# Another order for the hand-written statements of a fused cross-attention kernel: start, steady loop and end

## The chip, the core and the metric

The kernel runs on one core of a Trainium2 chip. The metric is the device time of one execution in microseconds (us); the median of three runs of the kernel before is 1369.0 us (1368.85 to 1369.27). Four compute engines matter: TensorE (PE: matrix products, with its weight loads shown apart as PEld), VectorE (DVE), ScalarE (ACT) and GpSimd (POOL). SyncE (SP) issues all the DMA transfers that are spoken of here. Each engine works through its own list of instructions in order and waits on semaphores for the others.

## What is computed

There are 64 independent batches, all in float32. In each, 256 rows of text `x` (512 wide) attend to 256 rows of context `c` (384 wide):

```python
text_p  = x @ W_text  + b_text              # 256 x 512
audio_p = c @ W_audio + b_audio             # 256 x 512
Q = layer_norm(text_p, g1, beta1)
K = layer_norm(audio_p, g2, beta2)
V = audio_p
alpha = softmax(Q @ K.T / sqrt(512))
h = (alpha @ V) @ W_out + b_out
out = layer_norm(h + x, g_out, beta_out)
```

## The kernel before, in words

**Work per batch.** The kernel saves products of matrices with Strassen-like schemes: blocks of the operands are added and subtracted ahead of the products, and the products are combined in PSUM. The sums that feed products are made on POOL, the combinations in PSUM on DVE and ACT. The weight W_out is folded into W_audio at the start (`fold_multiply`, `fold_evict`), so that `alpha @ c` is multiplied by one folded weight (`wao`).

Four kinds of work make up a batch:

- Keys: class `Thirds`, lines 559 to 731. The product of the context block and W_audio is cut into thirds and done as 15 products in five groups, `one()` to `five()`. Between them lie small steps in PSUM: after `one()`, ACT copies one result (`copy_n1`, line 608), DVE subtracts it from the other and leaves that in the bank of `T` (`start_t`, line 612), and only then can PE accumulate there (`three()`, line 595). Likewise `copy_t`, `start_l0` and `start_l1` stand between `three()` and `four()`, and `take_m` and `start_u` between `four()` and `five()`. `five()` accumulates in its third group of products on the `M0` that `start_u` has to have read.
- Queries: class `Pair`, lines 840 to 944, two batches at a time, with seven outer and seven inner products each. POOL makes the sums: `sum(1)` to `sum(4)` (line 857, 128x512 each), `side(m, 0)` (128x256), `side(m, 1)` and `side(m, 2)` (128x128; line 866).
- Scores and softmax: class `Attention`. `key_sums` and `query_sums` list the sums of the transposed keys and queries, `key_step(n)` and `query_step(n)` (lines 1016 and 1019) do them on POOL; `key_step(0)` is one 128x512 operation of POOL. Then `score_part`, `maxima`, `exponentials`, `reciprocals`, `divide_e`.
- Context and output: `context_part` and `context_two` (`alpha @ c`), then a second `Thirds` object, called `y` or `y1` in the loop, with the folded weight. It ends in `plus_ends`, `plus_middle`, `plus_n0` and the four sums `last_11`, `last_10`, `last_01`, `last_00` (lines 686 to 731) on DVE, which add `x` and leave totals for the layer norm of the output. That layer norm is `totals` (POOL), `deviation` (ACT), `shift` (DVE, line 1428), and `settle` (DVE, line 1439) for one half of the rows; the other half goes through `scale_row` (ACT) and `lift_rows` (POOL).

**Way through DRAM.** Normalised keys and queries and the exponentials are stored to DRAM (`store`, `store_e`), fetched back in squares of 32 (`fetch`, `fetch_e`) and transposed block by block on DVE (`turn`, `turn_e`). The inputs come in squares too (`load_c`, `load_x`) and are turned by `turn_c` and `turn_x`. The DMAs all stand in SP's list.

**Order.** Nothing schedules this kernel: it runs under a manual schedule, and the order of the Python statements is the order of the instructions on every engine. Lines 1482 to 2207 are the start (batches 0 to 3, with other forms of the same steps, among them class `Fork` for the queries), lines 2209 to 2569 the steady loop, and lines 2571 to 3050 the end (batches from 60 on). The loop `for b in range(4, B - 4, 2)` runs 28 times, and each round treats two batches at each stage of the pipeline; its first half is written with `k2`, `y`, `f`, `at`, `settled`, its second with `k21`, `y1`, `s`, `at1`, `settled1`. In the middle of a round, from line 2344 (`y.five()`) to line 2398 (`k21.three()`), the following stand among each other:

- on PE: `y.five()`, four `last.context_part`, `k21.one()`, two `s.multiply`, `k21.two()`, `old1.context_two(0)`, `s.multiply(1, 6)`, `k21.three()`;
- on DVE: `y.plus_ends`, `plus_middle`, `last_11`, `plus_n0`, `last_10`, `plus_middle`, `last_01`, `settled.settle(0)`, `y.last_00`, `k21.start_t()`;
- on POOL: `s.sum(1)`, `s.side(1, 0)`, `s.sum(2)`, `s.sum(3)`, `s.side(1, 1)`, `s.side(1, 2)`, `at1.query_step(0)`, `s.sum(4)`, and, after `k21.three()`, `att[b + 1].key_step(0)`.

The step that is spoken of most:

```python
def settle(self, t):
    nc.vector.scalar_tensor_tensor(
        self.y[:, t, :], self.y[:, t, :], self.r[t], beo_sb, ALU.mult, ALU.add
    )
```

Its two tensor inputs, the row `y` and `beo_sb`, lie in SBUF, as do those of `shift`. The small DVE steps of `Thirds` named above read at least one operand from PSUM.

Of the kernel before, what the change touches and what calls it, by code (L numbers as in the profile page):

```python
# [22 lines left out]
def kernel(  # L23
# [1525 lines left out]
    wa_blocks = third_weights(wa_sb, wa_t, [3])  # L1549
    xs_1 = SumX(xT.pop(1), nc.vector)  # L1550
    fold_multiply(0, 0, 1)
    centre(wt_sb, mean_wt, DC)
    xs[1] = xs_1
    wt_pairs = wt_blocks = weight_sums(wt_sb, DC // 2, 'wtsum')
    q[0].evict(1)
    g1_sb, be1_sb, g2_sb, be2_sb, bac_sb = take_columns()
# [3 lines left out]
    load_c(2)  # L1560
    q[1] = Fork(1, xs.pop(1).of, wt_blocks)
    k[1].evict(0)
    load_x(2)
    fold_multiply(0, 1, 2)
    load_c(3)
    fold_multiply(1, 1, 2)
    k[1].evict(1)
    third_weights(wa_sb, wa_t, [1], nc.vector)
    q[0].scales()
    Fork.seed()  # L1570
    k[1].square()
    cT[2] = turn_c(2)
    q[0].normalise([1])
    xs_1.add(1)
    q[0].normalise([0])
    fold_multiply(0, 2, 3)
    q[1].one()
    cs[2] = Sides(cT.pop(2), 'csum')
    xs_1.add(1)
    fold_multiply(0, 3, 4)  # L1580
    xT[2] = turn_x(2)
    k[1].scales()
    fold_evict(0)
    cs[2].add(1)
    third_weights(wa_sb, wa_t, [4], nc.vector)
    cs[2].add(1)
    q[1].seven()
    cs[2].add(1)
    load_x(3)
    q[1].after_one()  # L1590
    nc.vector.tensor_scalar(be2_sb, be2_sb, scale, None, ALU.mult)
    cT[3] = turn_c(3)
    cs[2].add(1)
    fold_multiply(1, 2, 3)
    q[0].store()
    q[1].two()
    cs[3] = Sides(cT.pop(3), 'csum')
    fold_multiply(2, 0, 1)
    cs[2].add(1)
    k[0].fetch()  # L1600
    ba_delta = third_bias(ba_sb, 'ba_delta')
    load_c(4)
    part = bias_parts()
    cs[2].add(1)
    cs[2].add(1)
    q[1].after_seven()
    cs[3].add(1)
    xs[2] = SumX(xT.pop(2))
    k[1].normalise([1])
    q[0].fetch()  # L1610
    q[1].six()
    k2_0 = k[2] = Thirds('k', 2, cs.pop(2), wa_blocks, ba_sb, ba_delta)
    q[1].after_six()
    inner_step(7, 0)
    fold_multiply(1, 3, 4)
    xs[2].add(1)
    fold_evict(1)
    k2_0.one()
    xs_1.add(1)
    k2_0.copy_n1()  # L1620
    Thirds.seed_with(ba_sb)
    q[1].five()
    bias_rest(part, 1, 2)
    nc.vector.tensor_scalar(g2_sb, g2_sb, scale, None, ALU.mult)
    k2_0.start_t()
    k[1].normalise([0])
    q[1].four()
    load_c(5)
    cs[3].add(1)
    q[1].after_five()  # L1630
    xs[2].add(1)
    k2_0.three()
    xs[2].add(1)
    at_0 = att[0] = Attention(0)
    cs[3].add(1)
# [48 lines left out]
    at_0.affine_keys(0)
    k[1].fetch()
    k2_0.copy_u()
    q[1].fetch()
    k2_0.leave_middle()
    at_0.affine_queries(2)
    nc.vector.tensor_tensor(both[:, 0], g1_sb, g2_sb, ALU.mult)  # L1690
    at_0.affine_queries(0)
    k2_0.middle_d()
    fold_bias(part)
    at_0.affine_queries(3)
    k2_0.leave_ends()
    q2_0.five()
    load_x(4)
    xs[3].add(1)
    k2_0.seed()
    k2_0.leave()  # L1700
    q2_0.after_five()
    k[1].turn([0])
    third_weights(wao_sb, wao_t, [1])
    at_0.affine_keys(2)
    k2_0.square(var_0[:, 2:], [0])
    cs[4] = Sides(cT.pop(4), 'csum')
    load_x(5)
    k2_1 = k[3] = Thirds('k', 3, cs.pop(3), wa_blocks, ba_sb, ba_delta)
    k2_0.middle_sum()
    at_0.score(0, 1)  # L1710
    k[1].turn([1])
    xs[3].add(1)
    q2_0.four()
    xs[3].add(1)
    q[3] = Fork(3, xs.pop(3).of, wt_blocks)
    k2_0.square(var_0[:, 2:], [1])
    k2_1.one()
    q2_0.two()
    cs[4].add(1)
    q2_1 = q[3]  # L1720
    k2_1.copy_n1()
    k2_1.start_t()
    q2_0.three()
    q[1].turn()
    xT[4] = turn_x(4)
    at_0.score(1, 2)
    cs[4].add(1)
    q2_0.square(var_0[:, :2], [0])
    at_0.score(2, 3)
    cs[4].add(1)  # L1730
    k2_1.three()
    at_0.score(3, 4)
    at_0.score(4, 5)
    q2_0.square(var_0[:, :2], [1])
    at_0.score(5, 6)
    at_0.score(6, 7)
    scales_of(q2_0, k2_0, var_0)
    q2_0.normalise([1])
    q2_0.normalise([0])
    load_c(6)  # L1740
    k2_1.two()
    cs[4].add(1)
    at_0.score(7, 8)
    last_1.maxima()
    q2_0.store()
    Fork.seed()
    cs[4].add(1)
    cs[4].add(1)
    at_1 = att[1] = Attention(1)
    k2_0.normalise([0])  # L1750
    k2_1.copy_t()
    k2_1.start_l0()
    k2_0.normalise([1])
    q2_1.seven()
    k2_1.start_l1()
    last_1.exponentials([0])
    q2_1.one()
    var = small.tile([P, 4], F32, tag="var4", name="var")
    at_1.affine_keys(3)
    inner_step(6, 0)  # L1760
    q2_1.after_one()
    inner_step(5, 0)
    k2_1.four()
    xs[4] = SumX(xT.pop(4))
    cs[4].add(1)
    k2_1.take_m()
    k2_0.store()
    last_1.exponentials([1])
    at_1.affine_keys(1)
    q2_0.fetch()  # L1770
    at_1.affine_queries(2)
    last_1.reciprocals()
    k2_2 = k[4] = Thirds('k', 4, cs.pop(4), wa_blocks, ba_sb, ba_delta)
    q2_1.six()
    at_1.affine_queries(0)
    q2_1.after_seven()
    xs[4].add(1)
    k2_1.start_u()
    k2_1.five()
    at_1.affine_keys(0)  # L1780
# [72 lines left out]
    at_1.reciprocals()
    at_2.affine_keys(1)
    at_2.affine_queries(2)
    k2_2.four()
    wao_blocks = third_weights(wao_sb, wao_t, [[0, 3], [4, 2]][1])
    xs[5] = SumX(xT.pop(5))
    k2_2.take_m()
    beo_sb = row(beta_out, 'beo')  # L1860
    old_2.context_two(0)
    load_x(6)
    old_2.context_two(1)
    inner_step(7, 2)
    old_2.copy_two()
    at_2.affine_queries(1)
    q2_2 = q[4]
    old_2.zsides.add(1)
    q2_2.one()
    q2_2.after_one()  # L1870
    at_2.affine_queries(0)
    settled, old, last = att.pop(0), att[1], att[2]
    k2_1.store()
    at_2.affine_keys(0)
    k2_2.start_u()
    q2_1.store()
    load_c_rows(1)
    k2_2.five()
    old_2.zsides.add(1)
    old_2.zsides.add(1)  # L1880
    q2_1.fetch()
    q2_2.seven()
    k2_2.copy_n()
    cT[6] = turn_c(6)
    at_2.affine_keys(2)
    q2_2.two()
# [1198 lines left out]
```

## Time and profile before

| | |
|---|---|
| median of 3 runs | 1369.0 us |
| the profiled execution | 1369.55 us |
| its span, first to last instruction | 1367.8 us |
| PE busy | 1341.2 us, 8839 products |
| DVE busy | 1236.8 us, 3191 instructions |
| ACT busy | 1209.4 us, 3391 instructions |
| POOL busy | 1192.1 us, 1745 instructions |
| granted TensorE clock | 0.999 |
| moved by DMA | 322.25 MB, mean 236 GB/s |

"Busy" is the union of an engine's instructions; matrix products overlap in a pipeline, so a product of float32 with 128 columns shows 275 ns although the next one starts after some 112 ns. Every float32 product shows as two records. A timeline row gives the start in us from the beginning of the span, the length, the engine, the line of the kernel, the operation, the operands (output<-inputs), the shapes and the count of merged instructions; in brackets stands the idle time of the engine before it and what ended it. The line is often that of a helper: L557 is every small DVE step in PSUM, L573 every product of a `Thirds`, so the operands tell them apart.

### The profile page before, as it was taken

To read this page: it belongs to the slowest core of one execution; us is meant where nothing else is said; L and a number is where in the kernel's file an instruction comes from. 1 tells how busy PE (TensorE), PEld (TensorE's weight loads), DVE (VectorE), ACT (ScalarE), POOL (GpSimd) and SP (SyncE) were. 2 spreads that over 40 slices of the span, in tenths; PEclk is the share of its full clock that TensorE was granted. 3 is DMA by queue.
4 is the path that set the end of the run, shared out by engine and by line. 5 is a ranking of instruction groups with operands and counts; after the bars stand their busy time and mean duration, and the time that the engine had idled before them with its cause. 6 is when DMAs were issued, how large, how long until landed. Compare 5 with 4: busy or idle time off the path is not lost.

```text
span 1367.8 us, 30175 instructions
## 1 busy us (share of the span) xinstructions
PE 1341.2 (98%) x8839; PEld 1249.3 (91%) x8839; DVE 1236.8 (90%) x3191; ACT 1209.4 (88%) x3391; POOL 1192.1 (87%) x1745
## 2 busy tenths in 40 slices
PE   9999999999999999999999999999999999999998
PEld 5798999999999999999999999999999999999986
DVE  6668999999999999999999999999999999999977
ACT  4888989999899989899989999989999898999895
POOL 5798988988998988988989889889889889889865
PEclk9999999999999999999999999999999999999999
DMA  9988788998888988889888889988889888889863
GB/s 217 232 235 229 211 226 241 250 248 233 225 254 245 253 244 238 225 251 233 247 257 233 233 239 250 244 239 238 235 239 252 243 241 228 247 238 242 244 214 130
DMA packets 448970, 322.25 MB, mean 236 GB/s; under 512 B 153765, under 2 KB 381349, under 8 KB 448806
## 3 DMA queue, kind: packets, MB, share of 16 engines
q1 hardware_dynamic: 448710, 320.20, 84.7%
q8 instruction: 71, 1.16, 0.4%
q14 instruction: 93, 0.76, 0.2%
q10 hardware_dynamic: 96, 0.13, 0.0%
HBM read 203.57 MB, written 116.65 MB: 234 GB/s over the span
## 4 chain that ended last, share of the span: by engine, by line
PE 73%; ACT 19%; issue 2%; DVE 2%; DMA 2%; POOL 1%; SPq 0%; DVEq 0%; ACTq 0%; POOLq 0%
PE ps_f L889 12%; PE ps_m L573 11%; PE ps_f L906 11%; PE ps_sc L1035 9%; PE ps_z L1175 8%; PE ps_n L573 7%; PE ps_u L573 7%; PE ps_l L573 4%; ACT junk L938 4%; ACT kr L504 3%; ACT qr L944 2%; ACT junk L476 2%; PE ps_f L749 2%; ACT e L1097 2%; PE ps_sc L974 1%
## 5 line engine op out<-in xcount | busy, mean ns | idle before, releaser
L368 POOL TENSOR_TENSOR csum<-csum,cT 128x256 f32<-128x256 f32 (+1 forms) x310 | 213.2, 696 | 7.4
L1175 PE MATMUL ps_z<-eT,c 128*128 128x256 f32 x768 | 196.8, 379 | 0.0
L873 POOL TENSOR_TENSOR xsums<-xsums 128x128 f32<-128x128 f32 (+1 forms) x261 | 143.6, 550 | 51.1 <-PE ps_f L889 48.5
L1175 PEld LDWEIGHTS ps_z<-eT,c 128*128 128x128 f32 x768 | 135.6, 190 | 10.3
L889 PE MATMUL ps_f<-wt_inner,xsums 128*128 128x128 f32 x696 | 137.2, 279 | 0.9 <-DVE ps_f L557 0.5
L543 ACT ACTIVATE qT<-qT,both 128x256 f32<-128x256 f32 x236 | 134.3, 593 | 0.0
L1035 PE MATMUL ps_sc<-kT,qT 128*128 128x128 f32 x928 | 131.9, 275 | 0.0
L1035 PEld LDWEIGHTS ps_sc<-kT,qT 128*128 128x128 f32 x928 | 121.4, 192 | 0.1
L889 PE MATMUL ps_f<-wtsum,xsums 128*128 128x128 f32 x696 | 120.3, 275 | 0.0
L889 PEld LDWEIGHTS ps_f<-wt_inner,xsums 128*128 128x128 f32 x696 | 111.9, 190 | 8.6 <-DVE ps_f L557 1.1
L906 PE MATMUL ps_f<-wt,X 128*128 128x256 f32 x464 | 114.6, 380 | 0.0
L889 PEld LDWEIGHTS ps_f<-wtsum,xsums 128*128 128x128 f32 x696 | 106.3, 191 | 6.0 <-DVE ps_f L557 0.7
L1431 DVE SCALAR_TENSOR_TENSOR yr<-yr,nm,go 128x512 f32<-128x512 f32 x124 | 109.6, 884 | 0.0
L1035 PE MATMUL ps_sc<-ksum,qsum 128*128 128x128 f32 x696 | 105.9, 275 | 0.0
L1035 PEld LDWEIGHTS ps_sc<-ksum,qsum 128*128 128x128 f32 x696 | 95.6, 192 | 1.4
L557 DVE TENSOR_TENSOR ps_l<-ps_m,t 128x171 f32<-128x171 f32 x248 | 84.0, 339 | 10.8 <-ACT t L621 3.0
L1241 ACT ACTIVATE junk<-yr,nm 128x512 f32<-128x512 f32 x124 | 89.8, 724 | 2.8 <-POOL nm L1223 1.8
L1020 POOL TENSOR_TENSOR qsum<-qT 128x256 f32<-128x256 f32 x118 | 86.6, 734 | 4.4 <-ACT qT L543 4.4
L504 ACT ACTIVATE kr<-kr,rstd 128x512 f32<-128x512 f32 x126 | 87.3, 717 | 1.9
L906 PEld LDWEIGHTS ps_f<-wt,X 128*128 128x128 f32 x464 | 81.5, 191 | 7.5
L1017 POOL TENSOR_TENSOR ksum<-kT 128x512 f32<-128x512 f32 x59 | 87.2, 1478 | 0.0
L368 POOL TENSOR_TENSOR csum<-cT 128x256 f32<-128x256 f32 (+1 forms) x124 | 86.0, 694 | 0.0
(322 smaller groups left out, 4666.0 us busy)
## 6 DMA issues: line engine op xcount, KB each, us to landing
kd<-kr SPq DMA_DIRECT2D x64, 512.0 KB, 3.8
qd<-qr SPq DMA_DIRECT2D x64, 512.0 KB, 2.8
kq<-kd SPq DMA_DIRECT2D x256, 128.0 KB, 3.4
qq<-qd SPq DMA_DIRECT2D x256, 128.0 KB, 3.3
xq<-in_x_dram SPq DMA_DIRECT2D x252, 128.0 KB, 3.7
x<-in_x_dram SPq DMA_DIRECT2D x63, 512.0 KB, 5.4
out_dram<-yr SPq DMA_DIRECT2D x62, 512.0 KB, 6.4
cq<-in_ctx_dram SPq DMA_DIRECT2D x252, 96.0 KB, 2.6
```

Of the source, the lines that this page charges most:

```text
L368: nc.gpsimd.tensor_tensor(*step)
L504: nc.scalar.mul(row, row, self.r[t])
L543: nc.scalar.activation(self.T[:, k, :], self.T[:, k, :], AF.Identity, bias=bet[:, k : k + 1], scale=gam[:, k : k + 1],)
L573: nc.tensor.matmul(place, lhsT=self.sides.of[n], rhs=self.weights[n], start=(n == 14), stop=True, skip_group_check=True,)
L873: nc.gpsimd.tensor_tensor(o, i0, i1, ALU.subtract)
L889: nc.tensor.matmul(self.place(m, i, j), lhsT=side, rhs=wt_parts[m][n], start=False, stop=True, skip_group_check=True)
L906: nc.tensor.matmul(bank[:, i], lhsT=self.sides[m][:, i, c], rhs=wt_pairs[m][c], start=False, stop=True, skip_group_check=True,)
L1017: nc.gpsimd.tensor_tensor(*self.ksteps[n])
L1035: nc.tensor.matmul(self.place(t, m), lhsT=self.qsides[n][:, c], rhs=self.ksides[n][:, c], start=False, stop=True, skip_group_check=True,)
L1175: nc.tensor.matmul(ps, lhsT=c_rows[self.b][:, s, bass.ts(j, P)], rhs=self.eT[:, s, :], start=start, stop=(s == ST - 1), skip_group_check=True,
L1241: nc.scalar.activation(junk, self.y[:, t, :], AF.Square, bias=self.nm[:, t : t + 1], accum_out=self.ssq[:, t : t + 1],)
L1431: nc.vector.scalar_tensor_tensor(row, row, self.nm[:, t : t + 1], go_sb, ALU.add, ALU.mult)
```

## The change

The statements of the start from line 1550 on, of the loop and of the end stand in another order. No statement is added, dropped or altered: the 360 statements of the loop are the same ones, 337 of them at another place, and buffers, transfers and shapes stay. The core of the diff, for what the prediction names (the middle of a round, the place before `k2.five()`, and the start):

```diff
@@ the loop, first half: between k2.four() and k2.five() @@
-        old.z_step(7)
+        cs[b + 3].add(1)
+        settled.shift(1)
+        at.open_scores()
+        at1.affine_both(0)
+        f.plus(5, 1)
+        f.multiply(5, 4)
+        settled.last_deviation()
+        k2.take_m()
+        settled.shift(0)
+        f.multiply(5, 3)
+        k2.start_u()
+        k2.five()
...
@@ the loop, the middle of a round, as it stands after @@
+        y.five()
+        last.context_part(0, 0)
+        at.maxima()
+        y.plus_ends(x_old)
+        s.side(1, 0)
+        last.context_part(1, 0)
+        y.plus_middle(x_old, 1)
+        y.last_11()
+        y.plus_n0()
+        s.sum(3)
+        s.side(1, 1)
+        s.sum(1)
+        s.sum(2)
+        y.last_10()
+        last.context_part(0, 1)
+        last.context_part(1, 1)
+        settled.settle(0)
+        y.plus_middle(x_old, 0)
+        k21.one()
+        y.last_01(x_old)
+        k21.copy_n1()
+        s.multiply(1, 1)
+        s.multiply(1, 7)
+        s.side(1, 2)
+        att[b + 1].key_step(0)
+        y.last_00()
+        s.sum(4)
+        k21.two()
+        old1.context_two(0)
+        at.reciprocals()
+        s.multiply(1, 6)
+        k21.start_t()
+        k21.three()
...
@@ the start, as it stands after @@
+    q[0].evict(1)
+    wt_pairs = wt_blocks = weight_sums(wt_sb, DC // 2, 'wtsum')
+    xs_1.add(1)
+    q[0].evict(0)
...
+    k[1].evict(1)
+    cT[2] = turn_c(2)
+    Fork.seed()
...
+    fold_multiply(0, 1, 2)
...
+    fold_multiply(1, 1, 2)
...
+    q[1].seven()
```

Among the DMAs of the loop, `load_x_rows(b - 1)` goes from the head of a round to its first half, `load_x(b + 6)` from the second half to the first, `k2.fetch` from before `k21.copy_n1` to after `k21.five`, and `at.store_e` to behind `q[b + 2].fetch`; `last.turn_e` (DVE) goes from behind `y.five` to before `y.four`.

More of the change, by code (lines that the diff above doesn't have):

```diff
@@ L1566 @@
+    cs[2].add(1)
     fold_multiply(1, 1, 2)
-    k[1].evict(1)
+    k[1].square()
     third_weights(wa_sb, wa_t, [1], nc.vector)
[L1569 to L1573, printed above, removed]
-    xs_1.add(1)
[L1575 to L1583, printed above, removed]
+    ba_delta = third_bias(ba_sb, 'ba_delta')
@@ L1584 @@
+    xs_1.add(1)
     cs[2].add(1)
     third_weights(wa_sb, wa_t, [4], nc.vector)
[L1586 to L1599, printed above, removed]
+    q[0].normalise([1])
     k[0].fetch()
-    ba_delta = third_bias(ba_sb, 'ba_delta')
@@ L1702 @@
-    k[1].turn([0])
-    third_weights(wao_sb, wao_t, [1])
+    cs[3].add(1)
     at_0.affine_keys(2)
[L1705 to L1708, printed above, removed]
     k2_0.middle_sum()
     at_0.score(0, 1)
-    k[1].turn([1])
[L1712 to L1718, printed above, removed]
-    cs[4].add(1)
@@ L1720 @@
[L1720 to L1732, printed above, removed]
+    q2_0.after_six()
+    k2_0.seed()
+    q2_0.five()
+    last_1 = att[0]
+    q2_0.four()
+    k[1].fetch()
+    cs[4] = Sides(cT.pop(4), 'csum')
+    q2_0.two()
+    var_1 = small.tile([P, 4], F32, tag='var4', name='var')
+    q2_0.after_five()
@@ L1861 @@
[L1861 to L1878, printed above, removed]
+    q2_2.after_one()
+    cs[5].add(1)
+    k2_2.five()
+    q2_2.seven()
+    q2_2.six()
@@ L1956 @@
-    old_2.o.start_u()
+    cs[5].add(1)
+    at_2.score(7, 8)
+    old_2.o.start_l0()
+    q2_2.square(var_2[:, :2], [1])
+    old_2.o.four()
+    scales_of(q2_2, k2_2, var_2)
+    att[3] = Attention(3)
+    at = att[3]
+    old_2.o.take_m()
+    var = small.tile([P, 4], F32, tag="var4", name="var")
+    q2_2.normalise([1])
+    k2_2.normalise([1])
+    xs[5].add(1)
+    old_2.o.start_u()
+    Fork.seed()
+    go_sb = row(g_out, 'go')
+    load_x(7)
+    old_2.o.five()
+    cs[5].add(1)
+    at_2.maxima()
@@ L2022 @@
-    k2.two()
-    q2.five()
-    k2.copy_t()
-    k2.start_l0()
-    k2.start_l1()
-    att[3].key_step(0)
-    at.query_sums()
+    k2.two()
+    old.copy_one()
+    k2.copy_t()
+    q2.after_six()
+    settled.totals()
+    k2.start_l1()
+    k2.start_l0()
+    q2_2.store()
+    old.copy_two()
+    settled.deviation(1)
+    q2.five()
+    settled.deviation(0)
+    old.z_step(0)
+    k2_2.fetch()
+    at.query_step(1)
+    k2.four()
+    at_2.divide_e([1])
+    at_2.store_e()
+    at.query_step(0)
@@ new lines @@
+        k2.copy_n1()
+        at.affine_both(1)
+        k2.start_t()
+        old.copy_two()
+        settled.totals()
+        f.multiply(5, 7)
+        f.spread(5)
+        f.keep(5)
+        if b + 4 < B: load_c(b + 4)
+        f.whole(4, 0)
+        k2.three()
+        old.copy_one()
+        q[b + 1].turn()
+        k2.copy_t()
+        f.multiply(5, 6)
+        at.affine_both(3)
+        f.plus(5, 0)
+        settled.deviation(1)
+        k2.two()
+        f.whole(4, 1)
+        att[b + 1] = Attention(b + 1)
@@ L2387 @@
-        s.side(1, 2)
-        k21.start_t()
+        s.sum(3)
+        k2.seed()
+        s.side(1, 1)
+        s.sum(1)
+        s.sum(2)
+        att[b + 1].key_sums()
+        y.last_10()
+        last.context_part(0, 1)
+        last.context_part(1, 1)
+        s.seed(1)
+        settled.settle(0)
+        at.exponentials([0])
+        y.plus_middle(x_old, 0)
+        k21.one()
+        y.last_01(x_old)
+        at.exponentials([1])
+        q[b + 2].store()
+        k21.copy_n1()
+        s.multiply(1, 1)
@@ L2454 @@
-        s.keep(6)
-        old1.z_step(4)
+        k2.fetch()
+        s.multiply(6, 7)
+        q[b + 3].store()
+        k21.copy_n()
+        s.keep(6)
+        cT[b + 4] = turn_c(b + 4)
+        at1.score_part(1, 7)
+        at1.query_step(1)
+        old1.z_step(4)
+        s.spread(6)
+        settled1.shift(1)
+        s.whole(2, 1)
+        k21.copy_u()
+        k21.leave_ends()
+        k21.leave_middle()
+        cs[b + 4] = Sides(cT.pop(b + 4), "csum").add(0)
+        k21.middle_v()
@@ new lines @@
+    k2.two()
+    var = small.tile([P, 6], F32, tag="var6", name="var")
+    old.product_sums()
+    f.multiply(5, 7)
+    at.query_sums()
+    at.affine_both(2)
+    k2.three()
+    f.side(5, 1)
+    at.affine_both(1)
+    k2.copy_t()
+    cT[B - 1] = turn_c(B - 1)
+    f.spread(5)
+    f.whole(4, 0)
+    f.keep(5)
+    q[B - 3].turn()
+    old.context_two(1)
+    settled.deviation(1)
+    cs[B - 1] = Sides(cT.pop(B - 1), "csum").add(0)
+    att[B - 3] = Attention(B - 3)
+    f.multiply(5, 6)
@@ L2914 @@
+    old.o.four()
+    settled_m3.store()
+    settled.shift(1)
+    last.start_products('csum', work, n=0)
+    at.reciprocals()
     old.o.take_m()
-    last.zsides.add(1)
-    settled_m3.store()
     old.o.start_u()
@@ L2919 @@
     at.context_two(0)
[L2920 to L2927 removed]
+    last.copy_two()
+    settled.shift(0)
+    q[B - 1].affine(g1_sb, be1_sb, [2])
+    at.context_one()
+    end = Attention(B - 1)
+    last.zsides.add(1)
+    old.o.plus_ends(x_rows[B - 4])
+    last.o.seed()
+    old.o.last_01(x_rows[B - 4])
+    old.o.plus_middle(x_rows[B - 4], 1)
@@ L2928 @@
+    last.zsides.add(1)
+    at.copy_one()
+    old.o.plus_n0()
+    k2_m3.fetch()
+    old.o.last_10()
+    settled.last_deviation()
+    last.zsides.add(1)
+    last.zsides.add(1)
+    last.o.two()
+    old.o.last_11()
+    at.context_two(1)
+    end.k.turn()
+    old.o.plus_middle(x_rows[B - 4], 0)
+    last_rows(B - 1)
+    old.o.last_00()
+    last.zsides.add(1)
+    last.o.one()
     at.copy_two()
+    end.affine_keys(0)
     last.zsides.add(1)
-    settled.last_deviation()
-    end = Attention(B - 1)
@@ L2932 @@
-    last.o.seed()
-    at.start_output()
-    old.o.last_10()
-    at.reciprocals()
-    at.copy_one()
-    last.zsides.add(1)
-    old.o.plus_middle(x_rows[B - 4], 0)
-    old.o.last_11()
-    settled.shift(0)
-    last.o.two()
-    last.zsides.add(1)
-    end.k.turn()
-    last.o.one()
-    old.o.last_01(x_rows[B - 4])
-    last.o.copy_n1()
-    at.multiply(0, bank[5])
-    end.affine_keys(0)
-    old.o.last_00()
-    end.score(0, 1)
-    end.start_output('kq')
-    end.affine_keys(3)
-    settled.settle(1)
@@ new lines @@
+    add_bias(B - 1, [1])
+    settled.settle(0)
+    last.o.copy_n1()
+    last.o.start_t()
+    settled.settle(1)
+    end.affine_keys(2)
+    old.deviation(0)
+    end.affine_keys(1)
+    last.o.three()
+    end.score(0, 1)
+    last.o.copy_t()
+    old.shift(0)
+    last.o.start_l1()
+    end.score(1, 2)
+    end.score(2, 3)
+    end.affine_keys(3)
+    last.o.start_l0()
+    old.deviation(1)
+    old.last_deviation()
+    old.shift(1)
+    last.zsides.add(1)
+    settled.store()
+    end.start_output('kq')
```

1906 lines of the change are left out of this document (896 added, 1010 removed).

## Prediction

> **What bounds the kernel now.** I read the page first, then the waits of PE, then the timeline of one round on each engine.
>
> ```profile
> span 1367.8 us, 30175 instructions
> PE 1341.2 (98%) x8839; PEld 1249.3 (91%) x8839; DVE 1236.8 (90%) x3191; ACT 1209.4 (88%) x3391; POOL 1192.1 (87%) x1745
> ```
>
> PE is busy for 98% of the span, so an order can gain only what PE loses between its products. The other three have about a tenth of idle time each, so none covers a delay of the others for long. How much PE loses is not seen in "busy", since overlapping products hide short gaps. I take the spacing of products that follow each other without a wait:
>
> ```profile
> 622.26 1.89 PE L1175 MATMUL ps_z<-eT,c 128*128 128x256 f32 x8
> 623.99 0.81 PE L573 MATMUL ps_n<-wa,csum 128*128 128x171 f32 x4
> ...
> 629.07 0.74 PE L573 MATMUL ps_m<-wa_thirds,csum 128*128 128x171 f32 x4
> 629.65 0.74 PE L573 MATMUL ps_l<-wa_thirds,cT 128*128 128x171 f32 x4
> ...
> 610.39 0.61 PE L1035 MATMUL ps_sc<-ksum,qsum 128*128 128x128 f32 x4
> 610.84 0.39 PE L889 MATMUL ps_f<-wtsum,xsums 128*128 128x128 f32 x2
> ```
>
> From start to start, 256 columns take 1.73/8 = 0.216 us, 171 columns 0.58/4 = 0.145, 128 columns 0.45/4 = 0.112. A round has 120 records of the thirds (4 objects with 15 products, two records each), 48 of 256 columns (12 for `whole`, 12 for the context, two each) and 112 of 128 columns (28 inner products of the queries, 28 of the scores, two each): 17.4 + 10.4 + 12.5 = 40.3 us. What a round takes, and where the rest goes:
>
> ```profile
> 599.75 0.51 DVE L557 TENSOR_TENSOR n<-ps_m,x 128x342 f32<-128x342 f32 x1 [0.29 <-PE ps_m L573]
> 601.48 0.33 DVE L557 TENSOR_TENSOR u<-ps_u,x 128x171 f32<-128x171 f32 x1
> 601.73 0.50 DVE L723 SCALAR_TENSOR_TENSOR yr<-ps_l,x 128x342 f32<-128x342 f32 x1
> 602.15 1.85 DVE L1440 SCALAR_TENSOR_TENSOR yr<-yr,rstd,beo 128x512 f32<-128x512 f32 x1
> 603.93 0.32 DVE L723 SCALAR_TENSOR_TENSOR yr<-ps_u,u 128x170 f32<-128x170 f32 x1
> 604.36 0.34 DVE L557 TENSOR_TENSOR ps_u<-ps_n,n 128x171 f32<-128x171 f32 x1
> ...
> 641.29 0.51 DVE L557 TENSOR_TENSOR n<-ps_m,x 128x342 f32<-128x342 f32 x1 [0.29 <-PE ps_m L573]
> ```
>
> The first and the last row are `y.plus_ends` of two rounds running: 641.29 - 599.75 = 41.54 us. A round loses 41.54 - 40.3 = 1.24 us, and 28 rounds lose 35 us. Nearly all of it is one wait:
>
> ```profile
> PE ps_u L573 <- DVE ps_u L557: 17.2, 28, 0.6
> ...
> 603.76 0.39 PE L889 MATMUL ps_f<-wt_inner,xsums 128*128 128x128 f32 x2
> 604.76 0.56 PE L573 MATMUL ps_u<-wa_thirds,csum 128*128 128x171 f32 x2 [0.61 <-DVE ps_u L557]
> 605.16 0.59 PE L1175 MATMUL ps_z<-eT,c 128*128 128x256 f32 x2
> ```
>
> It comes 28 times, once a round: `k21.three()` waits for `k21.start_t()`. The last product before it starts at 603.76 and takes 2 x 0.112, so `three()` could start at 603.98; it starts at 604.76, 0.78 late, and its two records take 0.40 instead of 0.29, 0.11 more. That is 0.89 of the 1.24 us, or 24.9 us in all rounds. The rest, 0.35 us a round, is spread over short gaps.
>
> The DVE rows say why `start_t` (604.36) is late. DVE starts `plus_ends` when PE releases it (599.75) and works without a break up to `start_t`; the one long row is `settled.settle(0)`, 1.85 us. Other rows of the same operation are far shorter, and POOL shows what the long one meets:
>
> ```profile
> L1440 DVE SCALAR_TENSOR_TENSOR yr<-yr,rstd,beo x62: 720/968/1879, 125.0 to 1344.9; 128x512 f32<-128x512 f32 x62
> ...
> 601.50 0.73 POOL L1020 TENSOR_TENSOR qsum<-qT 128x256 f32<-128x256 f32 x1
> 602.19 1.27 POOL L864 TENSOR_TENSOR X<-X,xsums 128x512 f32<-128x512 f32 x1
> 603.42 1.72 POOL L1017 TENSOR_TENSOR ksum<-kT 128x512 f32<-128x512 f32 x1
> ```
>
> The shortest, median and longest `settle` are 0.72, 0.97 and 1.88 us. The long one lies over POOL's `s.sum(4)` (602.19, next operation at 603.42), and DVE goes on at 603.93, 0.51 after POOL's next start, and the POOL operation that starts at 603.42 takes 1.72 us instead of about 1.28. So the two take turns: `settle` waits for the POOL operation in flight, then POOL's next one waits for `settle`. Which POOL operation is in flight when `settle` comes decides whether PE waits.
>
> **The change part by part.**
>
> *The middle of a round, 28 times.* PE's work from `y.five()` to `k21.three()` is the same list in nearly the same order, and so is DVE's between `plus_ends` and `start_t`: `settle` stands two steps earlier, behind `last_10`, and `reciprocals` is added. The order of POOL is new, and these are the rows to place it:
>
> ```profile
> 636.32 1.24 DVE L77 STREAM_TRANSPOSE X<-xq 128x1024 f32<-128x1024 f32 x1
> ...
> 637.70 1.28 POOL L864 TENSOR_TENSOR xsums<-X 128x512 f32<-128x512 f32 x1 [0.20 <-DVE X L77]
> 638.93 0.73 POOL L873 TENSOR_TENSOR xsums<-X 128x256 f32<-128x256 f32 x1
> 639.62 1.28 POOL L864 TENSOR_TENSOR xsums<-X,xsums 128x512 f32<-128x512 f32 x1
> 640.85 1.29 POOL L864 TENSOR_TENSOR xsums<-X 128x512 f32<-128x512 f32 x1
> ...
> 622.93 0.46 POOL L368 TENSOR_TENSOR csum<-csum,cT 128x128 f32<-128x128 f32 x1
> 623.35 0.46 POOL L368 TENSOR_TENSOR csum<-cT 128x128 f32<-128x128 f32 x1
> ```
>
> POOL starts its sums when `turn_x(b + 5)` ends, at 637.70, which is 641.29 - 637.70 = 3.59 before `plus_ends`; `turn_x` hangs on `y.one()`, and PE's list from there to `y.five()` is unchanged, so I keep that distance. Start to start, a 128x512 sum takes 1.23, a 128x256 one 0.69, a 128x128 one 0.42. In the new order `side(1, 0)`, `sum(3)`, `side(1, 1)`, `sum(1)`, `sum(2)`, `side(1, 2)` come first: 0.69 + 3 x 1.23 + 2 x 0.42 = 5.22, so `key_step(0)` starts 5.22 - 3.59 = 1.63 after `plus_ends`, in the frame of the rows above at 601.38; as `sum(2)` reads what `sum(1)` has just written, up to 0.1 later. `settle` takes the place behind `last_10`, 601.48. So `key_step(0)` is in flight first, by 0 to 0.1 us. It is of the size of the sums, so POOL's next start is at 601.43 + 1.23 = 602.66, and DVE goes on 0.51 later, at 603.17. Then come `plus_middle` (601.73 - 601.48 = 0.25), `last_01` (602.15 - 601.73 = 0.42), `last_00` to `start_t` (604.36 - 603.93 = 0.43, into whose gap `reciprocals` goes, with 0.03 over) and `start_t` to `three()` (604.76 - 604.36 = 0.40): 604.70. That is 0.06 earlier than 604.76, and 28 x 0.06 = 1.7 us gained.
>
> The Trainium skill, in SBUF — State Buffer, section "Who interferes with whom", says that a DVE operation with two SBUF inputs and a POOL operation that reads SBUF exclude each other, and that the one which starts first holds the ports for the whole instruction. The turns above agree with the first half. On the second, the rows have `settle` at 602.15 ahead of the sum at 602.19, and yet the sum went first; by the rule on these starts, the same 0 to 0.1 us would decide here.
>
> *Ahead of `k2.five()`.* `start_u` has to have read `M0` before the third product of `five()`:
>
> ```profile
> 630.11 0.74 DVE L1431 SCALAR_TENSOR_TENSOR yr<-yr,nm,go 128x512 f32<-128x512 f32 x1
> 630.76 0.34 DVE L557 TENSOR_TENSOR ps_u<-ps_m,m 128x171 f32<-128x171 f32 x1
> ...
> 630.68 0.75 PE L573 MATMUL ps_n<-wa_thirds,csum 128*128 128x171 f32 x4
> 631.26 0.74 PE L573 MATMUL ps_m<-wa_thirds,cT 128*128 128x171 f32 x4
> ```
>
> `start_u` ends at 631.10 and the third product starts at 631.26: a cover of 0.16 us today. The new order puts `z_step(3)` ahead of the two `shift`, and the sums of POOL against which the `shift` take turns are others. The `shift` at 630.11 frees DVE after 0.65, so it met nothing; against a POOL operation of 0.73 it may take up to 0.7 more, or nothing. Less the cover, the cost is 0 to 0.55 us a round; I take 0 for the likeliest case, the nearest row being this one, and keep the other end as a rival.
>
> *The rest of the loop.* `k21.one()` still follows `last_10` over the same products and keeps its short gap. The new neighbour of the round's end, `k2.one()` behind `last_10` of `y1`, has 7 groups of PE work (4 x 0.432 + 3 x 0.224 = 2.4 us) for a DVE chain that took 601.48 - 599.75 = 1.73 and has `plus_middle` (0.25) and two small steps more: about 2.2, hidden by 0.2. If a stretched `settle` ahead of it eats that, it costs a few tenths; this belongs to the rival with `shift`. `turn_e` before `y.four()` instead of after `y.five()` frees DVE time that ends in its wait for PE (0.29 at 599.75), so it brings nothing.
>
> *SP's list.* Transfers move past each other: `k2.fetch` goes behind `q[b + 2].store`, `at.store_e` behind a fetch of four issues, and `load_x(b + 6)` waits in front of `load_c(b + 5)` until `turn_x(b + 4)` has freed its buffer. The tightest way, store, fetch and turn of the exponentials, has this room today:
>
> ```profile
> 612.21 2.50 SPq L74 DMA_DIRECT2D eq<-ed x4
> ...
> 620.16 0.70 DVE L77 STREAM_TRANSPOSE eT<-eq 128x512 f32<-128x512 f32 x1
> ```
>
> The fetch is issued by 614.71 and turned at 620.16, 5.4 us later. I cost the moves at nothing under this cover; if it goes, DVE waits in front of the turn, and everything queued behind that on DVE with it, from `maxima` to the sums that PE waits for.
>
> *The start and the end.* The start loses two longer waits:
>
> ```profile
> 30.18 0.59 ACT L745 COPY ps_f<-bt 128x512 f32<-128x512 f32 x1 [1.35 <-DVE kr L465]
> ...
> 35.16 1.13 PE L749 MATMUL ps_f<-wt,X 128*128 128x256 f32 x4 [0.52 <-ACT ps_f L765]
> 41.63 0.53 PE L573 MATMUL ps_u<-wa_thirds,csum 128*128 128x171 f32 x2 [0.45 <-DVE ps_u L557]
> ```
>
> Both, 0.52 and 0.45 us and their slow first products, may go, since other work stands around them. But `q[1].seven()` now comes after only two `fold_multiply`, and it needs `Fork.seed`, which needs `k[1].evict(1)`; DVE has `xs_1.add(1)` in front of that in place of one eviction. So PE may wait there for up to about the 1.35 us that ACT waited for the same release, or for nothing. Bounds for the start: 1.5 gained to 1.5 lost, taken at 0. The end has the same products and the same last chain of layer norm; I take it at 0 with 1 us to each side.
>
> **The sum.** From the profiled execution's 1369.55 us (1.75 outside the span of 1367.8): 1369.55 - 1.7 = 1367.85. The median of the runs stands 0.55 lower, so the forecast is 1367.3, rounded 1367.0. Its own range is 1362 to 1373: 0.06 +- 0.1 us a round is 3 us to either side, and the start and the end add 2.5.
>
> **The rivals.** *Settle goes first (0.32).* If `settle` comes a tenth earlier against POOL, or POOL a tenth later, `key_step(0)` waits and `settle` takes its 0.72. Then `three()` could start at 601.48 + 0.72 + 0.25 + 0.42 + 0.43 + 0.40 = 603.70, before 603.98: the wait vanishes, and 28 x 0.89 = 24.9 us go. Some of it returns, since DVE then has less room elsewhere; I take 1.0 of it back: 1345, range 1341 to 1352. For it speaks that the margin is of the size of my rounding; against it, that in the old order the sum won although its row starts 0.04 after `settle`'s.
>
> *DVE is late at `start_u` (0.27).* The price is the stretch of a `shift` above the cover of 0.16 us, in front of `k2.five()` and, in the same way, of `y1.five()`; it decides from the point at which a `shift` or `settle` ahead of them meets a POOL operation with more than 0.16 us to run. At 0.35 us a round for both places together, a third of their 2 x 0.55, it is 28 x 0.35 = 9.8 us: 1367 + 10 = 1377, slower; range 1372 to 1384. For it: DVE is busy 90% and its stretches alone set the old wait. Against it: today's `shift` at that place met nothing.
>
> *The order changes nothing that PE sees.* Then 1369.0; this lies in the likeliest case's range, as the gain of 1.7 us is within what can be told.
>
> **How the numbers follow.** A measurement of this kernel can tell about 0.2%, 2.7 us, from no change. The likeliest case has 0.38: 0.12 faster, 0.21 within, 0.05 slower. The first rival's 0.32 is all faster; the second's 0.27 is 0.25 slower, 0.02 within; 0.03 is left for a wait that I do not see, slower. So faster 0.44, same 0.23, slower 0.33. The range leaves out about a tenth at the low end of the first rival and a tenth at the high end of the second: 1343 to 1379.
>
> **What would show it.** In the profile after, the row of PE waits for `ps_u` from DVE stays at 28 times and near 0.6 us each, and a long `settle` (about 1.7 us) lies over POOL's `ksum<-kT` of 128x512. If that row of waits is gone and the `settle` takes 0.7 to 1.0, the first rival holds. If new PE waits for `ps_m` behind DVE `ps_u` stand in `five()`, the second does. The forecast is wrong in its base if the rounds are equally long and the time differs: then the start or the end did it.

## The result, and the profile after

The new order takes 1390.7 us (median of 4 runs, 1390.2 to 1392.9), the old one 1368.9 (1368.8 to 1369.3): 1.62% slower, ratio 1.0162 with a 95% interval of 1.0144 to 1.0179. Nothing was added, and the granted clock is the same (0.999 and 1.000); the 21.8 us come from the order alone.

First the page after:

```profile
span 1388.4 us, 30050 instructions
...
PE 1356.2 (98%) x8839; PEld 1252.0 (90%) x8839; DVE 1257.2 (91%) x3191; ACT 1216.8 (88%) x3391; POOL 1185.4 (85%) x1745
```

PE and DVE are each "busy" longer, by 15.0 and 20.4 us, over the same instructions. An instruction that stands waiting inside its own record counts as busy. The share of PE, 98% before and after, tells nothing.

The waits of PE (us in total, times, longest):

```profile
PE ps_u L573 <- DVE ps_u L557: 20.9, 29, 1.1
```

This is the old wait, `k21.three()` behind `k21.start_t()`, 17.2 us before. It grew by 3.7 us, and no other row stands above 1.0 us. 28 of its 29 times are the rounds (0.74 us in the one shown below, 0.61 in the one of before); the 29th, 0.33 us, lies in the end. So this view misses most of the loss: it counts only time in which no product's record is open. The `settle` rows show more (shortest, median and longest in ns):

```profile
L1440 DVE SCALAR_TENSOR_TENSOR yr<-yr,rstd,beo x62: 741/1853/1877, 122.4 to 1361.4; 128x512 f32<-128x512 f32 x62
```

The median was 968 ns and is 1853: now both settles of a round are long. The timeline of DVE over one round (start, length):

```profile
691.45 0.51 DVE L557 TENSOR_TENSOR n<-ps_m,x 128x342 f32<-128x342 f32 x1 [0.47 <-PE ps_m L573]
...
693.17 1.85 DVE L1440 SCALAR_TENSOR_TENSOR yr<-yr,rstd,beo 128x512 f32<-128x512 f32 x1
694.95 0.32 DVE L557 TENSOR_TENSOR u<-ps_u,x 128x171 f32<-128x171 f32 x1
695.19 0.50 DVE L723 SCALAR_TENSOR_TENSOR yr<-ps_l,x 128x342 f32<-128x342 f32 x1
...
695.74 0.34 DVE L723 SCALAR_TENSOR_TENSOR yr<-ps_u,u 128x170 f32<-128x170 f32 x1
...
695.99 0.16 DVE L1107 RECIPROCAL rden<-den 128x2 f32<-128x2 f32 x1
696.18 0.34 DVE L557 TENSOR_TENSOR ps_u<-ps_n,n 128x171 f32<-128x171 f32 x1
...
709.38 1.87 DVE L1440 SCALAR_TENSOR_TENSOR yr<-yr,rstd,beo 128x512 f32<-128x512 f32 x1
711.17 0.29 DVE L557 TENSOR_TENSOR ps_f<-ps_f,i 128x128 f32<-128x128 f32 x1
711.37 0.32 DVE L557 TENSOR_TENSOR m<-ps_m,bao_delta 128x171 f32<-128x171 f32 x1
711.62 0.67 DVE L557 TENSOR_TENSOR v<-ps_f,v 128x512 f32<-128x512 f32 x1
712.21 0.33 DVE L557 TENSOR_TENSOR ps_u<-ps_m,m 128x171 f32<-128x171 f32 x1
...
733.79 0.51 DVE L557 TENSOR_TENSOR n<-ps_m,x 128x342 f32<-128x342 f32 x1 [0.47 <-PE ps_m L573]
```

From `plus_ends` to `plus_ends` a round takes 733.79 - 691.45 = 42.34 us, 0.80 more than the 41.54 before: 28 x 0.80 = 22.4, the whole loss. POOL beside the two settles:

```profile
693.21 1.27 POOL L1017 TENSOR_TENSOR ksum<-kT 128x512 f32<-128x512 f32 x1
694.44 1.72 POOL L864 TENSOR_TENSOR X<-X,xsums 128x512 f32<-128x512 f32 x1
...
709.02 0.45 POOL L368 TENSOR_TENSOR csum<-cT 128x128 f32<-128x128 f32 x1
709.43 1.27 POOL L1017 TENSOR_TENSOR ksum<-kT 128x512 f32<-128x512 f32 x1
```

The first settle (693.17) loses its turn to `att[b + 1].key_step(0)`, whose row starts 0.04 us later, the second (709.38) to `att[b + 2].key_step(0)`, 0.05 us later. In the old order the second settle came when that operation had just ended (617.39 + 1.27 = 618.66) and met short ones. The rows of before, DVE and then POOL:

```profile
618.67 0.95 DVE L1440 SCALAR_TENSOR_TENSOR yr<-yr,rstd,beo 128x512 f32<-128x512 f32 x1
```

```profile
617.39 1.27 POOL L1017 TENSOR_TENSOR ksum<-kT 128x512 f32<-128x512 f32 x1
618.62 0.46 POOL L873 TENSOR_TENSOR xsums<-xsums 128x128 f32<-128x128 f32 x1
```

And PE after, behind both:

```profile
695.45 0.39 PE L889 MATMUL ps_f<-wt_inner,xsums 128*128 128x128 f32 x2
696.58 0.56 PE L573 MATMUL ps_u<-wa_thirds,csum 128*128 128x171 f32 x2 [0.74 <-DVE ps_u L557]
...
710.82 0.61 PE L1035 MATMUL ps_sc<-kT,qT 128*128 128x128 f32 x4
711.51 0.49 PE L889 MATMUL ps_f<-wt_inner,xsums 128*128 128x128 f32 x2
711.84 0.75 PE L573 MATMUL ps_n<-wao_thirds,zsum 128*128 128x171 f32 x4
712.60 0.85 PE L573 MATMUL ps_m<-wao_thirds,zT 128*128 128x171 f32 x4
713.28 0.45 PE L573 MATMUL ps_u<-wao_thirds,zT 128*128 128x171 f32 x2
713.57 0.38 PE L889 MATMUL ps_f<-wtsum,xsums 128*128 128x128 f32 x2
713.80 1.13 PE L1175 MATMUL ps_z<-eT,c 128*128 128x256 f32 x4
...
715.26 1.03 PE L1175 MATMUL ps_z<-eT,c 128*128 128x256 f32 x4
```

Place one: `k21.three()` starts at 696.58 and could at 695.45 + 2 x 0.112 = 695.67. That is 0.91 late (0.78 before), and its records take 0.40 in place of 0.29, as before: 1.02 us in this round, 0.89 in the one of before. In most rounds the difference is a little smaller, 0.11: the idle time in brackets is mostly 0.72 or 0.73 us, and 0.61 or 0.62 before. Place two is new. `s.multiply(7, 5)` could start at 710.82 + 4 x 0.112 = 711.27 and starts at 711.51, when `s.plus(7, 0)` (711.17 + 0.29) is done; the third group of `y1.five()` could start at 711.84 + 0.58 = 712.42 and starts at 712.60, when `y1.start_u` (712.21 + 0.33) is done. With 0.10 for each restart that is 0.35 + 0.28. The context products at 713.80 take 0.10 more than the same at 715.26: by these rows place two costs 0.73 us a round. With the 0.11 of place one that makes 0.84; the rounds differ by 0.80. None of these waits of 0.2 us has an idle time in brackets, as the record of the product before is still open: they are seen only in starts.

### The profile page after: what moved, and what is told of

It is laid out like the page before. It is cut to its first block, busy times and chain, and to the rows that moved or that the text cites. A ratio compares the mean times of both kernels' runs of the same rounds, so it can differ in the third digit from the quotient of the medians.

```text
span 1388.4 us, 30050 instructions
## 1 busy us (share of the span) xinstructions
PE 1356.2 (98%) x8839; PEld 1252.0 (90%) x8839; DVE 1257.2 (91%) x3191; ACT 1216.8 (88%) x3391; POOL 1185.4 (85%) x1745
## 4 chain that ended last, share of the span: by engine, by line
PE 63%; DVE 28%; issue 4%; ACT 2%; DMA 1%; DVEq 0%; SPq 0%; ACTq 0%
PE ps_m L573 12%; PE ps_f L889 8%; PE ps_z L1175 8%; PE ps_f L906 7%; DVE yr L1440 7%; PE ps_n L573 7%; PE ps_sc L1035 7%; PE ps_u L573 6%; PE ps_l L573 4%; DVE yr L723 3%; DVE yr L1431 2%; DVE kT L536 2%; DVE qT L77 2%; DVE kr L557 2%; PE ps_f L749 2%
## 5 line engine op out<-in xcount | busy, mean ns | idle before, releaser
L1175 PE MATMUL ps_z<-eT,c 128*128 128x256 f32 x768 | 204.4, 383 | 0.0
L368 POOL TENSOR_TENSOR csum<-csum,cT 128x256 f32<-128x256 f32 x310 | 184.4, 607 | 7.1
L873 POOL TENSOR_TENSOR xsums<-xsums 128x128 f32<-128x128 f32 (+1 forms) x261 | 152.6, 585 | 5.2 <-PE ps_f L889 0.5
L543 ACT ACTIVATE qT<-qT,both 128x256 f32<-128x256 f32 x236 | 140.5, 596 | 0.0
L1035 PE MATMUL ps_sc<-kT,qT 128*128 128x128 f32 x928 | 136.6, 275 | 0.0
L1431 DVE SCALAR_TENSOR_TENSOR yr<-yr,nm,go 128x512 f32<-128x512 f32 x124 | 117.8, 950 | 17.0 <-ACT junk L1241 16.9
L889 PE MATMUL ps_f<-wtsum,xsums 128*128 128x128 f32 x696 | 125.7, 277 | 0.0
L1440 DVE SCALAR_TENSOR_TENSOR yr<-yr,rstd,beo 128x512 f32<-128x512 f32 x62 | 108.9, 1756 | 0.1
L1097 ACT ACTIVATE e<-ps_sc,nmx 128x256 f32<-128x256 f32 x128 | 58.8, 463 | 44.9 <-DVE nmx L1089 44.9
L536 DVE STREAM_TRANSPOSE kT<-kq 128x512 f32<-128x512 f32 x122 | 85.1, 698 | 1.9 <-DMA kq<-kd 1.9
```

Source lines behind the costliest of these rows:

```text
L368: nc.gpsimd.tensor_tensor(*step)
L536: nc.vector.transpose(self.T.rearrange("p k (q t j) -> p t q k j", t=self.nt, j=SQ)[:, t], self.sq[:, t * NQ : (t + 1) * NQ].rearrange("p ...
L543: nc.scalar.activation(self.T[:, k, :], self.T[:, k, :], AF.Identity, bias=bet[:, k : k + 1], scale=gam[:, k : k + 1],)
L873: nc.gpsimd.tensor_tensor(o, i0, i1, ALU.subtract)
L889: nc.tensor.matmul(self.place(m, i, j), lhsT=side, rhs=wt_parts[m][n], start=False, stop=True, skip_group_check=True)
L1035: nc.tensor.matmul(self.place(t, m), lhsT=self.qsides[n][:, c], rhs=self.ksides[n][:, c], start=False, stop=True, skip_group_check=True,)
```

## The experiments

Theory A: the loss is these two turns with POOL, and who goes first hangs on some hundredths of a microsecond. Its rivals: DVE's list is too long at place two by itself (B), start or end cost the time (C), `start_t` is late for another reason (D). Each run is timed beside the kernel before (1369.6 to 1369.9 us). "Round" is the median time from one `y.plus_ends` row to that of the next round.

| run | what differs | time, us | ratio to before (95%) | round, us |
|---|---|---|---|---|
| kernel before | | 1368.9 | | 41.56 |
| kernel after | | 1390.7 | 1.0162 (1.0144 to 1.0179) | 42.34 |
| e1_loop_only | new loop, old start and end | 1391.7 | 1.0160 (1.0145 to 1.0175) | 42.34 |
| e5_ends_only | old loop, new start and end | 1371.0 | 1.0012 (1.0003 to 1.0021) | 41.55 |
| e2_pool | after, second `key_step(0)` earlier | 1378.4 | 1.0061 (1.0046 to 1.0076) | 41.84 |
| e3_settle1 | after, second settle later | 1384.4 | 1.0110 (1.0095 to 1.0126) | 42.08 |
| e9_dummy2 | after, small POOL operation at place two | 1369.8 | 0.9999 (0.9990 to 1.0009) | 41.56 |
| e4_settle0 | after, first settle later | 1350.7 | 0.9860 (0.9843 to 0.9876) | 40.88 |
| e7_later | after, first settle later still | 1349.9 | 0.9857 (0.9842 to 0.9872) | 40.87 |
| e6_dummy | after, small POOL operation at place one | 1339.7 | 0.9780 (0.9765 to 0.9795) | 40.48 |
| e8_control | after, the same operation elsewhere | 1392.6 | 1.0165 (1.0150 to 1.0181) | 42.34 |
| b4_settle0 | before, first settle later | 1349.3 | 0.9853 (0.9837 to 0.9870) | 40.85 |
| b6_dummy | before, small POOL operation at place one | 1341.4 | 0.9791 (0.9775 to 0.9808) | 40.55 |

**Loop or ends.** e1_loop_only takes the loop of after and the rest of before, e5_ends_only the reverse.

> Start and end in the old order, the loop in the new one. Theory A (the loss is in the rounds): a round takes 42.34 us in the new order and 41.54 in the old, so 28 x 0.80 = 22.4 us above the kernel before, 1391 us. Rival C (the new start or the new end costs the time, the rounds only look longer): 1369 to 1375.

> Start and end in the new order, the loop in the old one. Theory A (the whole loss is in the rounds): 1368 to 1371 us, as the new start gained some 2 us of PE's gaps in the profile and the new end lost some 1.4. Rival C (start or end cost something): above 1373 us.

1391.7 and 1371.0: the loop carries the loss. The new start and end cost 1.3 us beside the old loop (1371.0 against 1369.7) and nothing that can be told beside the new one (ratios 1.0162 and 1.0160). Rival C is out.

**Place two, POOL's list alone.**

```diff
@@ e2_pool, against after @@
+        att[b + 2].key_step(0)
         s.side(7, 2)
...
-        att[b + 2].key_step(0)
```

> The new order, with one statement moved: att[b + 2].key_step(0), POOL's 128x512 operation, goes ahead of s.side(7, 2), so that settled1.settle(0) meets POOL operations of 128x128 (0.42 us apart) in place of one of 1.23. DVE's list is untouched. Theory A (the second settle of a round is long because it takes turns with the 128x512 operation of POOL): it falls from 1.87 to at most 0.72 + 0.42 = 1.14, DVE is 0.65 us or more earlier, and both waits of PE behind it go: 0.25 + 0.10 before multiply(7, 5), 0.17 + 0.10 in y1.five, 28 x 0.62 = 17.4 us: 1373 us. Rival B (DVE's list there is too long in the new order, with or without the turn): the waits stay, 1388 to 1391 us.

It gained 12.2 us, 0.50 a round, with DVE's list untouched. That speaks for A and against B, but it is less than expected (1378.4 us, not 1373). Its DVE and POOL rows say why:

```profile
704.36 1.38 DVE L1440 SCALAR_TENSOR_TENSOR yr<-yr,rstd,beo 128x512 f32<-128x512 f32 x1
```

```profile
703.92 1.27 POOL L1017 TENSOR_TENSOR ksum<-kT 128x512 f32<-128x512 f32 x1 [0.72 <-PE ps_sc L1035]
705.15 0.91 POOL L873 TENSOR_TENSOR xsums<-xsums 128x128 f32<-128x128 f32 x1
```

Moved up, the operation now waits (0.72, by its row for PE's score products) and is still in flight when the settle comes, 0.44 us into it. The settle takes 1.38, 0.49 less than in the kernel after; some of `y1.five`'s wait stays (by the starts of the products 0.14 of its 0.28).

**Place two, DVE's list alone.**

```diff
@@ e3_settle1, against after @@
-        settled1.settle(0)
         s.multiply(7, 7)
         y1.four()
...
         y1.start_u()
+        settled1.settle(0)
```

> The new order, with settled1.settle(0) behind y1.start_u instead of ahead of y1.four. Theory A: both waits of PE behind it go, 28 x 0.62 = 17.4 us: 1373 us, up to 5 more if the settle now delays the sums at the round's end. Rival B (raise_v ahead of start_u keeps start_u late by itself): only the wait before multiply(7, 5) goes, 28 x 0.35 = 9.8: 1381 us.

The settle fell to 0.74 and both waits went, so B's form of it, `raise_v` keeping `start_u` late, fell. But only 6.3 us came back: 1384.4 us, above what either theory forecast. A new row of PE waits says where the rest went:

```profile
PE ps_z L1175 <- DVE eT L77: 6.3, 28, 0.2
```

The settle now stands in front of `turn_e`, for which the context products wait, once a round. By the starts of the products that is about 0.5 us a round, of the 0.78 that the new order loses at this place.

**Place one, DVE's list alone.**

```diff
@@ e4_settle0, against after @@
-        settled.settle(0)
...
         k21.start_t()
+        settled.settle(0)
         s.seed(6)
```

> The new order, with settled.settle(0) behind k21.start_t instead of ahead of plus_middle. Theory A: the wait of k21.three (0.90 + 0.10 us a round) goes, 28 us: 1363 us; up to 6 us of it come back if the settle, still up to 1.85 us long at its new place, delays copy_t's followers. Rival D (start_t is late for another reason than the settle, such as PE's own product groups ahead of it): the wait stays, 1388 to 1391 us.

The same in the old order, and in the new one a step further back:

```diff
@@ b4_settle0, against before @@
-        settled.settle(0)
...
         k21.start_t()
+        settled.settle(0)
         k21.two()
@@ e7_later, against after @@
-        settled.settle(0)
...
         s.plus(1, 0)
+        settled.settle(0)
         old1.copy_one()
```

> The kernel before, with one statement moved: settled.settle(0) goes from behind last_01 to behind k21.start_t. Theory A (in the old order too, the settle alone makes start_t late): the wait of k21.three goes, 28 x 0.89 = 24.9 us: 1345 us, up to 5 more if the settle delays what follows at its new place. Rival D (the old loop has a floor of its own near 41.5 us a round, from DVE's list as a whole): 1366 to 1370 us.

> As the run that put settled.settle(0) behind k21.start_t in the new order (1350.7 us), but behind s.plus(1, 0). That run kept about 0.2 us a round before the product that waits for plus(1, 0), behind the settle. Theory A: that wait goes too, 28 x 0.2 = 6 us: 1345 us. Rival: the settle now delays start_l0 and start_l1 ahead of k21.four, or meets another 128x512 operation, and nothing is gained: 1350 to 1356 us.

The new order gained 40.0 us, 12 more than expected and 11 more than place one costs. Without the long first settle DVE comes to the second one earlier, and that one falls from 1.87 to 1.03: place two goes as well. What came back, about 0.4 us a round, are waits for `s.plus(1, 0)`, now behind the settle, and for `y1.start_t`. In the old order the same move gained 20.4 us of the 24.9, with a new wait of 0.2 + 0.1 us for `plus(1, 0)`. e7_later, with the settle behind `plus(1, 0)`, gained nothing to speak of (0.8 us where 6 were expected; its rival came true): that wait went, and others of about the same size stood in `k21.four` and before `y1.three`.

**Who goes first, by added work.** One operation on 128x1 elements, result unused, ahead of a 128x512 operation of POOL:

```diff
@@ e6_dummy, against after (e9_dummy2: ahead of att[b + 2].key_step(0); b6_dummy: before, ahead of s.sum(4); e8_control: ahead of settled.totals()) @@
+        late = small.tile([P, 1], F32, tag="late", name="late")
+        nc.gpsimd.tensor_scalar(late, nhalf[:, :1], 2.0, None, ALU.mult)
         att[b + 1].key_step(0)
```

> The new order, with work added: one operation of POOL on 128x1 elements (about 0.25 us, its result unused) ahead of att[b + 1].key_step(0), 28 times. POOL's 128x512 operation then starts 0.2 to 0.3 us after settled.settle(0) is ready, in place of 0.04. Theory A (which of the two comes first decides, within about 0.1 us): settle goes first and takes 0.75 to 1.0 in place of 1.85, start_t is 0.8 to 1.1 earlier, and the wait of k21.three goes: 28 x 1.00 = 28 us less, 1363 us, or down to 1350 if the second settle of the round then misses its 128x512 operation as well. Rival (the turn does not hang on so small a distance, or settle waits for the one in the queue anyway): no change or slower, 1390 to 1397 us.

> The new order with the same added operation of POOL (0.2 us, result unused, 28 times), but ahead of settled.totals(), where POOL stands idle for 2.11 us. Neither settle then meets anything else than before. Theory A (only the shift against the settle counts): 1389 to 1393 us. Rival (an added small operation helps or hurts by itself): clearly below 1385 or above 1396 us.

> The new order with the same added operation ahead of att[b + 2].key_step(0), the 128x512 operation that the second settle of a round meets 0.05 us after its own start. Theory A: that settle goes first, its two waits behind it go (0.62 us a round), the first settle and the wait of k21.three stay: 28 x 0.62 = 17.4 us less, 1373 us. Rival B (DVE's list is too long there by itself): 1386 to 1392 us.

> The kernel before, with the same added operation of POOL ahead of s.sum(4), whose 128x512 operation starts 0.04 us after settled.settle(0). Theory A: settle goes first, the wait of k21.three goes, 28 x 0.89 = 24.9 us: 1345 us. If the two orders are equal but for what the settles meet, it should come out at the 1339.7 us of the new order with the operation ahead of key_step(0). Rival (the old order meets another wait): 1355 to 1372 us.

More work, 28 times 0.2 us, made the kernel 51 us faster than the kernel after, more than the 28 to 41 expected. DVE and POOL at place one of e6_dummy, and DVE at its second settle:

```profile
711.70 0.76 DVE L1440 SCALAR_TENSOR_TENSOR yr<-yr,rstd,beo 128x512 f32<-128x512 f32 x1
712.38 0.32 DVE L557 TENSOR_TENSOR u<-ps_u,x 128x171 f32<-128x171 f32 x1
...
726.71 0.75 DVE L1440 SCALAR_TENSOR_TENSOR yr<-yr,rstd,beo 128x512 f32<-128x512 f32 x1
```

```profile
711.72 0.22 POOL L2386 TENSOR_SCALAR late<-nhalf 128x1 f32<-128x1 f32 x1
711.89 1.71 POOL L1017 TENSOR_TENSOR ksum<-kT 128x512 f32<-128x512 f32 x1
```

`key_step(0)` starts 0.19 us after the settle in place of 0.04. Now the settle goes first with 0.76 and POOL pays (1.71 in place of 1.27). A round takes 40.48 us against the 40.3 that PE needs. The same operation where POOL is idle changes nothing (e8_control, 42.34 us a round), so the shift did it, not the operation. At place two alone it gives 0.78 us a round (e9_dummy2), a little more than the 0.73 read from the rows; expected was 0.62, without the slow context products. In the old order it gives 28.5 us (b6_dummy), 1.01 a round; expected was 24.9.

The kernel before holds one such case without any edit. One of its 28 waits of PE for `ps_u` is the one at 41.63 us, in the start, so one of the 28 rounds has none. In that round the settle went first; DVE, POOL and PE of the kernel before:

```profile
392.95 0.51 DVE L557 TENSOR_TENSOR n<-ps_m,x 128x342 f32<-128x342 f32 x1 [0.29 <-PE ps_m L573]
...
395.35 0.75 DVE L1440 SCALAR_TENSOR_TENSOR yr<-yr,rstd,beo 128x512 f32<-128x512 f32 x1
...
433.51 0.51 DVE L557 TENSOR_TENSOR n<-ps_m,x 128x342 f32<-128x342 f32 x1 [0.29 <-PE ps_m L573]
```

```profile
395.41 1.83 POOL L864 TENSOR_TENSOR X<-X,xsums 128x512 f32<-128x512 f32 x1
```

```profile
396.96 0.39 PE L889 MATMUL ps_f<-wt_inner,xsums 128*128 128x128 f32 x2
397.19 0.46 PE L573 MATMUL ps_u<-wa_thirds,csum 128*128 128x171 f32 x2
```

`three()` starts right behind the product before it (397.19 - 396.96 = 0.23), and the round takes 433.51 - 392.95 = 40.56 us, as a round of b6_dummy does. POOL's row starts 0.053 us behind the settle's; in the other 27 rounds it is 0.031 to 0.064, and POOL went first.

## Why the prediction was wrong

The forecast was 1367.0 (1343 to 1379), and it came to 1390.7.

- **The bound** was read rightly. PE's 40.3 us a round is the floor that e6_dummy nearly reaches (40.48).
- **The middle of a round**: the mechanism was right, the placing and a size were off. The prediction had `key_step(0)` "in flight first, by 0 to 0.1 us". In the rows it starts 0.04 behind the settle and went first all the same, so that this part came true is in part luck. The wait stays, and the long settle lies over `ksum<-kT`. But `three()` was forecast 4.95 us behind `plus_ends` and came 696.58 - 691.45 = 5.13. DVE went on 0.08 later than forecast (694.95 - 691.45 = 3.50, not 3.42), because `key_step(0)` itself started that much later (693.21 - 691.45 = 1.76, where the prediction reckoned with 1.68). The way from `last_01` to `last_00` was costed at 0.42, from a row of before in which the settle stood between them; directly behind each other it took 695.74 - 695.19 = 0.55. `reciprocals` fitted into its gap as costed: 0.44 from `last_00` to `start_t`, 0.43 before. In place of 0.06 gained it was about 0.1 lost.
- **Ahead of `k2.five()`**, taken at 0: right. No wait of PE stands there after.
- **The rest of the loop** is the step that failed. It priced `k21.one()`, `k2.one()` and `turn_e`, and never placed the second settle against POOL. That settle had moved from behind `y1.four()` to ahead of it, and `att[b + 2].key_step(0)` to within 0.05 us of it. The settle that meets POOL was worked out to hundredths at one place, and its twin 16 us later was not looked at. What was put at nothing there cost 0.78 us a round (e9_dummy2), 28 x 0.78 = 21.8 us.
- **The rival "DVE is late at `start_u`"** had the mechanism: a stretched `shift` or `settle` ahead of `y1.five()`, with PE behind it. Its price of 0.35 us a round, "a third of their 2 x 0.55", was a guess between bounds. Place two measured 0.78, with a second product, `multiply(7, 5)`, waiting too, which no part had named. At 28 x 0.78 = 21.8 us the rival would have come out at 1367 + 22 = 1389.
- **The rival "settle goes first"** was not what happened, but its price is borne out in the main: where the settle is made to go first, the time is 1339.7 in the new order and 1341.4 in the old. Forecast was 1345 (1341 to 1352), with 0.89 a round where it is 1.01 in the old order, and with 1.0 us given back that was not. The prediction read the 28 waits of before as one a round; in fact one round had none, and its 40.56 us would have shown how near the tie was and what it is worth.
- **SP's list**, costed at nothing: right. With the two turns gone a round of the new order has 0.2 us left for everything else, transfers among it.
- **Start and end**, taken at 0 with 2.5 us of bounds: within 1.3 us, right.

The Trainium skill, in SBUF — State Buffer, section "SBUF: two separate sides", says that of a DVE operation with two SBUF inputs and a POOL operation that reads SBUF the one which starts first gets the shared ports for the whole instruction, and that the other is blocked. The lengths bear this out both ways: 1.85 us for the settle where POOL was first, 0.76 and a POOL operation of 1.71 where the settle was. The starts of the rows don't tell which was first at such distances: POOL's two rows of the kernel after start 0.04 and 0.05 us behind the settles', and POOL had the turn.

The fastest version is e6_dummy, the new order with one small operation added: 2.2% below the kernel before. Free of the turn at place one, the new order (1339.7) and the old (1341.4) differ little. So nearly all of what was measured as the worth of an order was the worth of two meetings, 0.04 and 0.05 us apart.

## What to carry to other kernels

List every DVE operation with two inputs in SBUF that PE waits behind, and place each of them against POOL's long operations, not only the one that hurts today; a stall taken early moves the later ones. Where a few hundredths of a microsecond decide such a turn, an order can't be judged by its time alone: shift POOL or DVE by a small operation or a moved statement and see whether the time jumps. And read PE's losses from the starts of its products, since neither its busy share nor its waits showed the new one.

## What the runs showed of the hardware

- The length of a settle follows from the POOL operation ahead of it: 0.74 + (end of that row - start of the settle's row) - 0.2. The kernel after: 694.48 - 693.17 - 0.2 + 0.74 = 1.85, measured 1.85; e2_pool: 705.19 - 704.36 - 0.2 + 0.74 = 1.37, measured 1.38. Here 0.74 is the length of a settle that meets nothing; so where POOL goes first, the settle's own work begins some 0.2 us before the end that POOL's row shows.
- Rows don't show which was first when they start almost together. In the rounds of the kernel before POOL's row starts 0.03 to 0.06 us after the settle's, and POOL went first in 27 of them and DVE in one. In e3_settle1 the second settle meets another operation of POOL (`kT<-kT,ksum`, 128x256) whose row starts 0.05 to 0.07 us after, and DVE went first all 28 times (settle 0.74 to 0.75). With 0.10 to 0.25 us, in e6_dummy, DVE went first. So rows 0.05 to 0.06 us apart have gone either way.
- A 128x1 operation of POOL that starts 0.02 us after the settle costs it next to nothing (0.76 in place of 0.74).
